# Attention's softmax sums: folded by small transfers and summed in the turn to queries, instead of by matmuls with ones

## The chip, the cores and the metric

The kernel runs on one core of a Trainium2 chip. The metric is the device time of one execution in microseconds (us), the median of several runs. The core has five engines that run side by side and meet through semaphores: TensorE (PE: matmuls, with PEld for its weight loads), VectorE (DVE), ScalarE (ACT), GpSimd (POOL) and SyncE (SP, which here only issues transfers). Each engine works through its own instructions strictly in order: an instruction that waits holds up all behind it. POOL and SP also issue transfers (DMAs), which 16 DMA engines carry out; a transfer that adds to its destination (an accumulate) is issued by POOL. SBUF is the working memory of 128 partitions, PSUM the memory that PE writes.

## The reference, cut to what matters

Two graph layers run one after the other over 16 batches of 1024 nodes with 256 features and a mask `adj`. The change touches the first one, attention with 8 heads of 32 features:

```python
normed = layer_norm(x, gamma1, beta1)
qkv = normed.reshape(b_, n_, H, HD).transpose(0, 2, 1, 3)
scores = jnp.einsum('bhqd,bhkd->bhqk', qkv, qkv) * scale
masked = jnp.where(adj_matrix[:, None, :, :] > 0, scores, -jnp.inf)
attn = jax.nn.softmax(masked, axis=-1)
out = jnp.einsum('bhqk,bhkd->bhqd', attn, qkv)
```

The softmax divides by a sum over 1024 keys. The kernel computes exp(scores) without division, weighs the values with it, and divides at the end by the sum. An MLP (1024 wide, GELU) and the second layer (single-head attention over the same mask, ELU) follow; together they are the "rest" below. All arithmetic that matters here is float32.

## The kernel before, in words

**Tiles.** In `attention` one batch is 32 *units*: 2 blocks of 512 queries (`qh`) x 2 sets of four heads (`g`) x 8 key tiles of 128 keys (`kt`). The eight units of one `(qh, g)` are called a *group* here, and a batch has four groups. In a unit `scores` lets PE write scores transposed, keys on the partitions and 4 heads x 512 queries along the row, into two PSUM tiles `sc0` and `sc1` (L990). These have one buffer each, so PE's next scores need DVE to have read the last ones. DVE adds the mask (L1011) and writes tile `e`, 128 x 2 x 512, once for each pair of heads; ACT takes the exponential (L1014). A unit later PE multiplies `e` with the values into `o` (`weigh`, L1027). At the last key tile DVE copies `o` to SBUF (L1042).

**The sums.** The first key tile's two `e` tiles are the accumulators `acc` (pool `accp`, two buffers each). For each further key tile `add_up` adds `e` to them by an accumulating DMA from POOL's queue (L1051), 512 KB each, two a unit. `e` tiles come from `ep`, with five buffers: one is free again when its accumulate has landed. After the last key tile each partition of `acc` holds a partial sum over 8 keys. `total` sums over the partitions: a matmul with ones gives, for head j, the sum in 32 rows of a PSUM tile `den` (L929), and ACT copies it to `ds` (L937). One unit later `invert` turns it to queries on partitions by small matmuls of `ds` with `each_head`, a matrix that picks one row of every 32 (L947), and DVE takes the reciprocal (L951). `finish` transposes `o` (L961) and DVE multiplies (L963). POOL adds the result to the residual `h` (L967). `finished[b, qh]` counts this.

In batch 0 PE adds the mask for two heads itself, and odd key tiles are summed by DVE in tiles `odd`; that path is not touched.

**The order of the work.** The order is written out by the program itself while it records instructions. Several generators ("streams") yield places on a common scale of batches, and the one with the lowest place goes next: attention (`stream_a`), the rest of the batch before (`stream_b`, one step of 1.75 us of PE work at a time), prologue, masks, set-up. `clock` is the program's own account of PE time. `defer(us, f)` records f once the clock has gone that far, which puts its instructions at that place in their engines' orders; it is no wait on the chip. `go_on` runs once a unit and hands each finished group on, a unit at a time: weighed, summed (`total`), totalled (`invert`). `turns` is a list of short PE jobs that are put in between steps.

`rest` does MLP and second layer in chunks of 256 queries: `expand` (ph, DVE L1184, GELU L1191), `contract` (po, L1211), then the second layer (`weights`: lg, DVE L1281 and L1286, ACT L1287; `attend`: pa, L1324 to L1334). The second half's chunks need `finished[b, 1]`; until then stream B yields without work. PSUM tiles other than `sc` and `o` share three buffers (`psm`).

**Other work on the queues.** POOL also computes `nrm` and `va` for the next batch (L815, L816), the small powers `rs` that DVE's normalisations need (L745), and the residual adds (L1127, L1128). SP issues all loads, the mask's transposes (L902) and the stores. DVE turns the loaded mask into FP8 (L592).

Of the kernel before, what the change touches and what calls it, by code (L numbers as in the profile page):

```python
# [9 lines left out]
F32 = mybir.dt.float32  # L10
# [4 lines left out]
ALU = mybir.AluOpType  # L15

P = 128
# [477 lines left out]
def fast_path(  # L495
# [28 lines left out]
    nc = tc.nc  # L524
    B, N, D = x.shape
    DFF = W1.shape[1]
    H, HD = 8, D // 8
    GH = 4
# [4 lines left out]
    QW = 512  # L533
# [7 lines left out]
    pool = lambda name, bufs, **kw: ctx.enter_context(tc.tile_pool(name=name, bufs=bufs, **kw))  # L541
    const = pool("const", 1)
# [6 lines left out]
    midp = pool("midp", 3)  # L549
    ep = pool("ep", 5)  # L550
    accp = pool("accp", 2)
    lp1 = pool("lp1", 6)
    tmpp = pool("tmpp", 2)
    smallp = pool("smallp", 3)
# [45 lines left out]

    each_head = const.tile([P, GH], F32, name="each_head")
    nc.vector.tensor_copy(each_head, ident[:, ::HD])
    ident8 = const.tile([P, P], FP8, name="ident8")
    nc.vector.tensor_copy(ident8, ident, saturate=False)
    ones = const.tile([P, HD], F32, name="ones")
# [152 lines left out]
    def defer(us, f):  # L758
        deferred.append((clock[0] + us, len(deferred), f))

        return clock[0] + us
# [160 lines left out]
    scored, weighed, summed, totalled = [], [], [], []  # L922

    def total(b, qh, g, os, accs):

        den = ps_tile([P, QW], f"den_{b}_{g}_{qh}")
        for j in range(GH):
            for acc in accs:
                nc.tensor.matmul(  # L929
                    den[j * HD : (j + 1) * HD, :],  # L930
                    ones,
                    acc[j // 2][:, j % 2, :],
                    start=acc is accs[0],
                    stop=acc is accs[-1],
                )
        ds = tmpp.tile([P, QW], F32, tag="w2", bufs=3, name=f"ds_{b}_{g}_{qh}")
        nc.scalar.copy(ds, den)  # L937
        totalled.append((b, qh, g, ds, os))

    finished = {}  # L940

    def invert(b, qh, g, ds, os):

        pt = ps_tile([P, TPH, GH], f"ptds_{b}_{g}_{qh}")
        for t in range(TPH):
            for c in range(0, P, HD):
                nc.tensor.matmul(  # L947
                    pt[c : c + HD, t, :], ds[:, t * P + c : t * P + c + HD], each_head, start=True, stop=True
                )
        rl = smallp.tile([P, TPH, GH], F32, tag="rl", name=f"rl_{b}_{g}_{qh}")  # L950
        ready = defer(1.0, lambda: nc.vector.reciprocal(rl, pt))  # L951
        turns.append((1, lambda: finish(b, qh, g, rl, ready, os)))
# [16 lines left out]
    def attention(b, st):  # L969
        va, kT = st["va"], st["kT"]  # L970

        def scores(qh, g, kt):
            qs = slice(qh * QW, (qh + 1) * QW)
            sc = [
                psc.tile([P, 2, QW], F32, tag=f"sc{i}", name=f"s_{b}_{g}_{qh}_{kt}_{i}") for i in range(2)
            ]

            by_pe = 2 if b == 0 else 0  # L980
            if by_pe:
                for j in range(by_pe):
                    matmul(
                        sc[j // 2][:, j % 2, :], ident8, st[qh][:, kt // 2, :, kt % 2], start=True, stop=False
                    )
                clock[0] += 0.45
            for j in range(GH):
                r = slice(j * HD, (j + 1) * HD)
                for c in range(0, P, P // 2):
                    nc.tensor.matmul(  # L990
                        sc[j // 2][c : c + P // 2, j % 2, :],
                        kT[r, g, kt * P + c : kt * P + c + P // 2],
                        kT[r, g, qs],
                        start=j >= by_pe,
                        stop=True,
                    )
            mb = st[qh][:, kt // 2, :, kt % 2].unsqueeze(1).to_broadcast([P, 2, QW])
            es = []
            if b == 0 and kt % 2:

                odd = midp.tile([P, 2, 2, QW], F32, tag="mid", name=f"odd_{g}_{qh}_{kt}")
            for i in range(2):
                if b == 0 and kt % 2:
                    e = odd[:, i]
                elif kt == 0:
                    e = accp.tile([P, 2, QW], F32, tag=f"acc{i}", name=f"acc_{b}_{g}_{qh}_{i}")
                else:
                    e = ep.tile([P, 2, QW], F32, tag="e", name=f"e_{b}_{g}_{qh}_{kt}_{i}")
                masked = sc[i]
                if 2 * i >= by_pe:  # L1010
                    nc.vector.tensor_tensor(e, masked, mb, op=ALU.add)  # L1011
                    masked = e
                es.append(e)
                weights = lambda e=e, masked=masked: nc.scalar.activation(e, masked, AF.Exp, scale=SCALE)  # L1014
                if i == 0:
                    weights()
            return es, weights

        acc = {}


        def weigh(qh, g, kt, es):
            if kt == 0:
                acc[g, qh] = pso.tile([P, QW], F32, tag="o", name=f"o_{b}_{g}_{qh}")
            o = acc[g, qh]
            for j in range(GH):
                nc.tensor.matmul(  # L1027
                    o[j * HD : (j + 1) * HD, :],
                    va[:, kt, (g * GH + j) * HD : (g * GH + j + 1) * HD],
                    es[j // 2][:, j % 2, :],  # L1030
                    start=(kt == 0),
                    stop=(kt == NT - 1),
                )
            if b == 0 and kt % 2:

                if kt > 1:
                    for n, (e, w) in enumerate(zip(es, odds[g, qh])):
                        defer(1.0 + 2.5 * n, lambda e=e, w=w: nc.vector.tensor_add(e, e, w))
                odds[g, qh] = es
            if kt == NT - 1:  # L1040
                c = tmpp.tile([P, QW], F32, tag="w2", bufs=3, name=f"os_{b}_{g}_{qh}")
                nc.vector.tensor_copy(c, o)  # L1042
                weighed.append((b, qh, g, c, [s[g, qh] for s in (sums, odds) if s]))

        sums, odds = {}, {}


        def add_up(qh, g, kt, e, i):
            if b == 0 and kt % 2:
                return  # L1050
            nc.gpsimd.dma_start(sums[g, qh][i], e, accum_op=ALU.add)  # L1051

        units = [(qh, g, kt) for qh in range(NQH) for g in range(NG) for kt in range(NT)]
        for u in units:
            make_turns()
            es, rest_of_weights = scores(*u)
            go_on()
            rest_of_weights()
            qh, g, kt = u
            if kt == 0:  # L1060
                sums[g, qh] = es
            else:
                for i in range(2):
                    defer(2.0 + 1.5 * i, lambda u=u, e=es[i], i=i: add_up(*u, e, i))
            scored.append((weigh, (*u, es)))
            yield
# [47 lines left out]
    def rest(b, st, tails):  # L1114
# [55 lines left out]
        def expand(c):  # L1170
            yield from wait_for(turn, c)
            hid = midp.tile([P, FC, CW], F32, tag="mid", name=f"hid_{b}_{c}")
            for f0 in range(0, FC, 2):
                ph = ps_tile([P, 2, CW], f"ph_{b}_{c}_{f0}")
                for i in range(2):
                    for dc in range(DC):
                        matmul(
                            ph[:, i, :],
                            w1[:, dc, (f0 + i) * P : (f0 + i + 1) * P],
                            yT[c][:, dc, :],  # L1180
                            start=(dc == 0),
                            stop=(dc == DC - 1),
                        )
                nc.vector.tensor_tensor(  # L1184
                    hid[:, f0 : f0 + 2, :],
                    ph,
                    b1c[:, f0 : f0 + 2].unsqueeze(2).to_broadcast([P, 2, CW]),
                    op=ALU.add,
                )
                yield 1.75, True  # L1190
            return hid, defer(1.0, lambda: nc.scalar.activation(hid, hid, AF.Gelu))  # L1191
# [153 lines left out]
        hid = {0: (yield from expand(0))}  # L1345
        ask(turn, 1)
        yield from tails[b]()
        while finished.get((b, 1), 0) < NG:
            yield 0.0, None
        prepare(b, st, 2)  # L1350
        load(2)
        hid[1] = yield from expand(1)
        ask(turn, 2)
        prepare(b, st, 3)
        yield from contract(0, hid[0])
        load(3)
        hid[2] = yield from expand(2)
        ask(turn, 3)
# [135 lines left out]
    while any(p is not None for p in places):  # L1494
        i = min((p, i) for i, p in enumerate(places) if p is not None)[1]
# [69 lines left out]
```

## Time and profile before

| what | value |
|---|---|
| median of 3 runs | 3469.32 us (3466.48 to 3476.8) |
| the profiled execution: its own time | 3465.53 us |
| its span, first to last instruction | 3463.8 us |
| mean granted PE clock | 0.998 |
| PE / DVE / ACT / POOL busy | 99% / 79% / 54% / 41% |
| accumulates acc<-e | 864 of 512 KB, median 6.2 us from issue to landing |
| matmuls den<-acc | 512 instructions, 592 ns each, several at once |

Reading the rows: a group of the profile has line, engine, operation, what it writes and reads, and the count; behind the bar stand busy us and mean ns of one, then how long the engine sat idle before, and what ended that. One float32 matmul of the program appears as two instructions, and a matmul with 32 columns of weights runs beside three others, so durations of single matmuls don't add up: PE's time is read from the start of one set to the start of the next. Line numbers are those of the kernel before.

### The profile page before, as it was taken

Reading aid. Unit: us, or ns where it says so; the run is one execution under the profiler, and the core shown is the slowest. Engines: PE = TensorE matmul, PEld = TensorE weight load, DVE = VectorE, ACT = ScalarE, POOL = GpSimd, SP = SyncE. Lnnn points to the kernel's source line nnn. Section 1 sums busy time; section 2 is a strip of 40 time slices with the busy share of each in tenths; the row PEclk is TensorE's granted clock in tenths of the full one; section 3 lists DMA queues with packets and bytes.
Section 4 is the critical chain, followed back from the end, with each engine's and each line's share of the span. In section 5 each row is a group of like instructions: output and inputs, shape, how many; then the busy total and the mean of one; then the engine's idle time right before and its main releaser. Section 6 shows DMA issues by size and latency. Waiting matters only on the chain. (4 is left out here: it accounts for less than half of the span.)

```text
span 3463.8 us, 119015 instructions
## 1 busy us (share of the span) xinstructions
PE 3421.5 (99%) x52478; PEld 1644.7 (47%) x52478; DVE 2751.4 (79%) x5194; ACT 1857.5 (54%) x2184; POOL 1416.9 (41%) x1708
## 2 busy tenths in 40 slices
PE   7999999999999999999999999999999999999998
PEld 2344444444444444444444444444444444444477
DVE  6888788787878878888887887878878788887754
ACT  5555555555555555555555555555555555555522
POOL 4443443434444344443444434344343443433220
PEclk9999999999999999999999999999999999999999
DMA  8799989999899998999999899998999989899730
GB/s 195 154 183 181 185 164 194 177 193 185 164 185 176 185 187 169 184 171 191 189 177 186 166 189 179 188 187 168 186 178 193 186 163 184 170 193 180 153 64 14
DMA packets 281902, 598.56 MB, mean 173 GB/s; under 512 B 94880, under 2 KB 130080, under 8 KB 281376
## 3 DMA queue, kind: packets, MB, share of 16 engines
q0 software_dynamic: 124416, 453.04, 71.5%
q1 hardware_dynamic: 156672, 137.56, 15.9%
q8 instruction: 414, 6.78, 0.8%
q14 instruction: 112, 0.92, 0.1%
q10 hardware_dynamic: 288, 0.26, 0.0%
HBM read 104.21 MB, written 16.78 MB: 35 GB/s over the span
## 5 line engine op out<-in xcount | busy, mean ns | idle before, releaser
L1014 ACT ACTIVATE e<-e 128x1024 f32<-128x1024 f32 x852 | 895.9, 1057 | 947.6 <-DVE e L1011 715.3
L1051 POOL DMA_DIRECT2D acc<-e x864 | 756.2, 891 | 1447.4 <-DMA acc<-e 664.6
L1011 DVE TENSOR_TENSOR e<-s,mk 128x1024 f32<-128x1024 f32 x852 | 1004.0, 1218 | 180.1 <-PE s L990 148.4
L990 PE MATMUL s<-kT 32*64 32x512 f32 x8192 | 577.3, 615 | 2.9 <-DVE odd L1011 2.9
L1027 PE MATMUL o<-e,va 128*32 128x512 f32 x3456 | 462.9, 606 | 2.1 <-ACT e L1014 2.1
L571 PE MATMUL pa<-gw,e 128*32 128x258 f32 x7648 | 454.3, 380 | 0.6 <-issue 0.6
L571 PE MATMUL lg<-fT,uT 128*32 128x256 f32 x7680 | 448.5, 379 | 0.0
L571 PE MATMUL ph<-yT,w 128*32 128x256 f32 x7808 | 448.5, 379 | 0.0
L571 PE MATMUL po<-w,hid 128*32 128x256 f32 x7680 | 440.5, 379 | 0.0
L571 PEld LDWEIGHTS ph<-yT,w 128*32 128x32 f32 x7808 | 259.8, 110 | 197.7 <-issue 42.5
L571 PEld LDWEIGHTS po<-w,hid 128*32 128x32 f32 x7680 | 250.2, 110 | 209.1 <-issue 61.6
L571 PEld LDWEIGHTS lg<-fT,uT 128*32 128x32 f32 x7680 | 258.4, 110 | 190.1 <-issue 38.9
L571 PEld LDWEIGHTS pa<-gw,e 128*32 128x32 f32 x7648 | 249.9, 110 | 202.5 <-issue 49.9
L1287 ACT ACTIVATE e<-e,shift 128x512 f32<-128x512 f32 x256 | 183.0, 717 | 186.0 <-DVE e L1286 161.2
L1281 DVE SCALAR_TENSOR_TENSOR e<-lg,gw,mk 128x256 f32<-128x256 f32 x512 | 223.2, 478 | 71.6 <-PE lg L571 61.1
L1184 DVE TENSOR_TENSOR hid<-ph,b1c 128x512 f32<-128x512 f32 x256 | 175.6, 688 | 85.6 <-PE ph L571 74.2
L1027 PEld LDWEIGHTS o<-e,va 128*32 128x32 f32 x3456 | 68.8, 108 | 354.0 <-issue 219.9
L1286 DVE SCALAR_TENSOR_TENSOR e<-e 128x512 f32<-128x512 f32 x256 | 196.6, 768 | 8.8
L1014 ACT ACTIVATE acc<-acc 128x1024 f32<-128x1024 f32 x124 | 131.0, 1057 | 129.0 <-DVE acc L1011 124.6
L990 PEld LDWEIGHTS s<-kT 32*64 32x64 f32 x8192 | 120.6, 130 | 162.8 <-issue 105.0
L1011 DVE TENSOR_TENSOR acc<-s,mk 128x1024 f32<-128x1024 f32 x124 | 146.1, 1218 | 20.8 <-PE s L990 20.6
L815 POOL TENSOR_TENSOR nrm<-nrm,g 128x256 f32<-128x256 f32 x128 | 113.3, 885 | 60.9 <-DVE nrm L749 60.9
(146 smaller groups left out, 3817.9 us busy)
## 6 DMA issues: line engine op xcount, KB each, us to landing
acc<-e POOLq DMA_DIRECT2D x864, 512.0 KB, 6.2
adj<-in_adj_dram SPq DMA_DIRECT2D x248, 256.0 KB, 5.6
h<-in_x_dram SPq DMA_DIRECT2D x64, 256.0 KB, 6.3
xb<-in_x_dram SPq DMA_DIRECT2D x128, 128.0 KB, 4.2
out_dram<-z SPq DMA_DIRECT2D x128, 128.0 KB, 4.0
adj<-in_adj_dram SPq DMA_DIRECT2D x4, 512.0 KB, 7.1
mk<-mq SPq DMA_TRANSPOSE x128, 6.4
w<-in_L_gnn_W_dram SPq DMA_DIRECT2D x2, 1024.0 KB, 9.6
```

Of the source, the lines that this page charges most:

```text
L571: nc.tensor.matmul(out[c : c + HD], lhsT[:, c : c + HD], rhs, start=start, stop=stop)
L815: nc.gpsimd.tensor_mul(nrm, nrm, g1)
L990: nc.tensor.matmul(sc[j // 2][c : c + P // 2, j % 2, :], kT[r, g, kt * P + c : kt * P + c + P // 2], kT[r, g, qs], start=j >= by_pe, stop= ...
L1011: nc.vector.tensor_tensor(e, masked, mb, op=ALU.add)
L1014: weights = lambda e=e, masked=masked: nc.scalar.activation(e, masked, AF.Exp, scale=SCALE)
L1027: nc.tensor.matmul(o[j * HD : (j + 1) * HD, :], va[:, kt, (g * GH + j) * HD : (g * GH + j + 1) * HD], es[j // 2][:, j % 2, :], start=(kt = ...
L1051: nc.gpsimd.dma_start(sums[g, qh][i], e, accum_op=ALU.add)
L1184: nc.vector.tensor_tensor(hid[:, f0 : f0 + 2, :], ph, b1c[:, f0 : f0 + 2].unsqueeze(2).to_broadcast([P, 2, CW]), op=ALU.add,)
L1281: nc.vector.scalar_tensor_tensor(e[:, j, :], lg[:, j, :], gw[:, kt, D : D + 1], st[c // 2][:, kt // 2, qs, kt % 2], op0=ALU.add, op1=ALU.add,)
L1286: nc.vector.scalar_tensor_tensor(e, e, ALPHA, e, op0=ALU.mult, op1=ALU.max)
L1287: ready = defer(2.5, lambda: nc.scalar.activation(e, e, AF.Exp, bias=shift))
```

## The change

For the groups of batches 1 to 14 and of the first query block of batch 15 (58 of 64), `total` is no longer called. `fold` takes its place. In `acc[0]` the lower 64 partitions get the upper 64 added, in `acc[1]` the other way round, each by one accumulating DMA of 64 partitions from POOL (`fold_halves`). Then each head's 32 partitions of a tile `part` are filled from its own quarter (`take_own`, four DMAs of 32 x 512 from SP) and get the other quarter added (`add_other`, four accumulating DMAs from POOL). `part` then holds 32 partial sums a head, and `invert` uses it in place of `ds`, with `head_of` in place of `each_head`: ones on the head's 32 rows, so that the small matmul that turns to queries also sums. The steps are deferred by 5, 12, 17 and 23 us of the program's clock.

In the same groups the second key tile (`kt == 1`) is added to `acc` by a POOL tensor add instead of a DMA. And in `rest` the second `expand` stands ahead of the wait for `finished[b, 1]`, and two pieces of the first `contract` ahead of the turn of chunk 2.

```diff
+    foldp = pool("foldp", 1)
...
+    head_of = const.tile([P, GH], F32, name="head_of")
+    nc.gpsimd.memset(head_of, 0.0)
+    for j in range(GH):
+        nc.gpsimd.memset(head_of[j * HD : (j + 1) * HD, j : j + 1], 1.0)
...
-        totalled.append((b, qh, g, ds, os))
+        totalled.append((b, qh, g, ds, os, each_head))
+
+    def folds(b, qh):
+        return 0 < b and (b < B - 1 or qh == 0)
+
+    def fold(b, qh, g, os, acc):
+
+        part = foldp.tile([P, QW], F32, tag="part", name=f"part_{b}_{g}_{qh}")
+        half = [slice(i * P // 2, (i + 1) * P // 2) for i in range(2)]
+        heads = [slice(j * HD, (j + 1) * HD) for j in range(GH)]
+
+        def fold_halves():
+            for i in range(2):
+                nc.gpsimd.dma_start(acc[i][half[i]], acc[i][half[1 - i]], accum_op=ALU.add)
+
+        def take_own():
+            for j in range(GH):
+                nc.sync.dma_start(part[heads[j]], acc[j // 2][heads[j], j % 2, :])
+
+        def add_other():
+            for j in range(GH):
+                nc.gpsimd.dma_start(part[heads[j]], acc[j // 2][heads[j ^ 1], j % 2, :], accum_op=ALU.add)
+
+        defer(5.0, fold_halves)
+        defer(12.0, take_own)
+        defer(17.0, add_other)
+        defer(23.0, lambda: totalled.append((b, qh, g, part, os, head_of)))
...
-    def invert(b, qh, g, ds, os):
+    def invert(b, qh, g, ds, os, head):
...
-                    pt[c : c + HD, t, :], ds[:, t * P + c : t * P + c + HD], each_head, start=True, stop=True
+                    pt[c : c + HD, t, :], ds[:, t * P + c : t * P + c + HD], head, start=True, stop=True
...
-                weighed.append((b, qh, g, c, [s[g, qh] for s in (sums, odds) if s]))
+                if folds(b, qh):
+                    fold(b, qh, g, c, sums[g, qh])
+                else:
+                    weighed.append((b, qh, g, c, [s[g, qh] for s in (sums, odds) if s]))
...
+            if kt == 1 and folds(b, qh):
+                nc.gpsimd.tensor_add(sums[g, qh][i], sums[g, qh][i], e)
+                return
             nc.gpsimd.dma_start(sums[g, qh][i], e, accum_op=ALU.add)
...
         yield from tails[b]()
+        hid[1] = yield from expand(1)
         while finished.get((b, 1), 0) < NG:
             yield 0.0, None
         prepare(b, st, 2)
         load(2)
-        hid[1] = yield from expand(1)
+        pieces = contract(0, hid[0])
+        yield next(pieces)
+        yield next(pieces)
         ask(turn, 2)
         prepare(b, st, 3)
-        yield from contract(0, hid[0])
+        yield from pieces
         load(3)
```

## The prediction, made before the result was known

> **What bounds the kernel now.** I read the page first, then PE's waits, then one batch's window, then short timelines of PE, GpSimd (POOL) and VectorE (DVE).
>
> ```profile
> PE 3421.5 (99%) x52478; PEld 1644.7 (47%) x52478; DVE 2751.4 (79%) x5194; ACT 1857.5 (54%) x2184; POOL 1416.9 (41%) x1708
> q0 software_dynamic: 124416, 453.04, 71.5%
> L1051 POOL DMA_DIRECT2D acc<-e x864 | 756.2, 891 | 1447.4 <-DMA acc<-e 664.6 <-ACT e L1014 446.6 <-issue 86.8
> ```
>
> Since a busy PE is not yet a bounding PE, the list of its waits decides:
>
> ```profile
> PE ptk L823 <- POOL va L816: 18.8, 4, 15.9
> PE s L990 <- DVE odd L1011: 2.9, 2, 2.0
> PE s L571 <- ACT acc L1014: 2.5, 2, 1.4
> ```
>
> Below these stand only entries of 2.1 us and less, so PE waits some 33 us in 3463.8, nearly all in the first batch. From then on every cut of PE work is worth its full length, until something makes PE wait. One batch is 216.1 us, 54.0 for each of its four groups (a group: one block of 512 queries, four heads, eight key tiles):
>
> ```profile
> 1787.55:2003.60 216.05, 216.05 (x3452) 102.17 (x3448) 178.00 (x332) 119.34 (x140) 90.76 (x110) 1.00 0.94 182
> ```
>
> The columns are PE, PEld, DVE, ACT and POOL busy, the granted clock, the DMA engines' busy share and GB/s. PE never pauses, the clock is full, but DVE is at 178 of 216 and the DMA engines are at 0.94: two resources stand close behind PE. The POOL row of the page shows why the second matters: 664.6 us of POOL's idle time is waiting for one accumulate (L1051) to land before the next into the same tile.
>
> **Part 1: the sums' matmuls (removed).** The changed program has total() only for the six groups that do not fold; 14 batches x 4 + 2 = 58 groups lose theirs. The cost is read from start to start:
>
> ```profile
> 682.13 1.06 PE L1027 MATMUL o<-e,va 128*32 128x512 f32 x8
> 683.01 1.04 PE L929 MATMUL den<-acc,ones 128*32 128x512 f32 x8
> 683.87 1.48 PE L571 MATMUL lg<-fT,uT 128*32 128x256 f32 x24
> ```
>
> 683.87 - 683.01 = 0.86 us, all on the path. 58 x 0.86 = 49.9 us gained. The copy of den on ACT (567 ns each) goes too and is worth nothing, ACT being 55% busy. The matmuls of invert() and finish() stay, one unit later (key tile 4 instead of 3): 0. The five new memsets at the start: under 0.5 us (the row of such a memset is 0.1), 0 taken.
>
> **Part 2: the new order in rest().** In the changed program's PE order only one pair of expand matmuls and the turn pty of chunk 2 move by a unit. They fill the place that ptds and ptos leave; PE's work is the same: 0. If the cover were gone, it would cost what PE waits for the second sums, which is part 4.
>
> **Part 3: the second key tile on POOL.** 58 x 2 = 116 accumulates become tensor adds of 128x1024. POOL's adds of 256 columns average 750 ns (L1128), those of 512 have a median of 1286, so 1024 take about 1286 + 2 x 536 = 2.36 us. POOL has the time (275 us more on 1417); the question is DVE.
>
> ```profile
> L1286 DVE SCALAR_TENSOR_TENSOR e<-e x256: 691/692/2056, 260.0 to 3446.7; 128x512 f32<-128x512 f32 x128
> L967 POOL TENSOR_TENSOR h<-h,ot x64: 1266/1286/2274, 67.3 to 3325.7; 128x512 f32<-128x512 f32 x64
> ```
>
> These are minimum, median and maximum. L1286 reads SBUF alone; where a POOL add runs beside it, it takes up to 2056 ns and the POOL op stretches too, while L1011, which reads PSUM, stays at 1218 throughout. So a 2.36 us add can hold L1286, L592, L1333 and L1334 for up to its length. The worst place that I found is the group (second queries, second heads):
>
> ```profile
> 1794.11 0.69 DVE L1286 SCALAR_TENSOR_TENSOR e<-e 128x512 f32<-128x512 f32 x1
> 1794.72 0.76 DVE L592 TENSOR_SCALAR mq<-adj 128x512 fp8e5<-128x512 int32 x2
> 1795.39 2.35 DVE L1011 TENSOR_TENSOR e<-s,mk 128x1024 f32<-128x1024 f32 x2
> ```
>
> With adds from about 1792.7 to 1798, L1286 slips in between them and L592 waits for the second. L1011 then starts near 1798.4 and ends near 1800.8. PE's next scores, which need it, started at 1800.31 and would now start 0.86 earlier: a PE wait of 1.3 us. In the group (first queries, first heads) no such DVE op falls under the adds: 0. (Second queries, first heads): 0 to 2, by whether a small DVE op gets in before the first add. (First queries, second heads): 0. So 1.3 to 3.3 us a batch.
>
> **Part 4: the fold closes a loop on POOL.** Today the first accumulate of a group goes to a fresh tile and waits for nobody's landing:
>
> ```profile
> 1749.26 0.85 POOL L1051 DMA_DIRECT2D acc<-e  x1 [1.69 <-ACT e L1287]
> 1752.85 0.85 POOL L1051 DMA_DIRECT2D acc<-e  x1 [2.73 <-ACT gw L1263]
> 1755.59 0.85 POOL L1051 DMA_DIRECT2D acc<-e  x1 [1.90 <-DMA acc<-e]
> ...
> 1785.61 0.86 POOL L1051 DMA_DIRECT2D acc<-e  x1 [2.43 <-DMA acc<-e]
> 1791.36 0.86 POOL L1051 DMA_DIRECT2D acc<-e  x1 [4.89 <-ACT e L1014]
> ```
>
> 1749.26 is the second accumulate of key tile 2, 1785.61 that of key tile 7: five steps in 36.35 us, 7.3 each, of which the landing of the step before takes 6.2 in the median (4.5 at least, 11.6 at most). In the changed order POOL waits, after key tile 7, for its landing; then issues the folds of halves, makes both adds, issues key tile 2's first accumulate, four add_other (which wait for SP's take_own, and that for the folds), and only then key tile 2's second accumulate. The loop is:
>
> - five steps 36.35 + last landing 6.2 = 42.5;
> - second fold 0.9, adds 4.7, one accumulate 0.9, four add_other at the row's 0.86 = 3.4: 9.9;
> - ordinary POOL work standing between them (none, one h/xb pair of 1.8, two pairs with a small pow of 0.7, four nrm/va with one): 0, 1.8, 4.3 and 4.3, mean 2.6;
> - sum 55.0 us a group, against PE's 54.0 - 0.86 = 53.1.
>
> So PE would wait 1.9 a group, at ptds, or where DVE wants an e tile that has not been added. The bounds: the small DMAs' issue is shown nowhere on POOL; SP's issues take 0.34, so four at that price (1.4 for 3.4), with landings at the 4.5 minimum and 0.5 from a landing to the next, make 5 x 5.0 + 4.5 + 7.9 + 2.6 = 40.0, no wait at all. Upward, the group (first queries, first heads), with more loads under way, needed 44.3 instead of 42.5 by the same reading: 56.8 in all, 3.7 a group. I take 1.2: nearest to the measured 55.0, less a part for the two accumulates a group that no longer crowd the engines (the 256 KB folds and 64 KB pieces move the same bytes, 1024 KB, but in POOL's pause). Part 3's waits lie in the same groups, before ptds, and are contained in it: a PE that has waited at the scores finds the sums landed. 58 x 1.2 = 70 us lost.
>
> SP's queue: take_own stands before h loads, transposes and stores, and holds them some 4 us; their use is more than a unit (5.5 us) away: 0, and if not, DVE would wait at L592.
>
> The Trainium skill speaks against the small transfers: "DMA: Bandwidth & Descriptors", Rules for kernel authors, has transfers under 64 KB as mostly overhead. Its section Anatomy of one DMA gives 2.0 us + bytes/436e3, an estimate of 3.2 us for 512 KB where this trace's median is 6.2; by it the loop would be near 34 us and nothing would be lost. The measured landing decides.
>
> **The sum.** -49.9 + 70 = +20 on the profiled execution (3465.5 us; span 3463.8 and 1.7 around it): 3485.6. The median of the runs lies 3.8 above that execution: 3489.
>
> **Rivals.**
> - *The loop closes in time* (faster). Small DMAs cost POOL little and landings shorten, the loop stays under 53; only DVE's blocks are left, 14.5 batches x 1.3 to 3.3 = 19 to 48, of which I count 15, because DVE's 38 idle us of a batch let it catch up where POOL's adds start early: -49.9 + 15 gives 3434 beside the median, from 3420 with nothing lost. For it: the DMA engines idle in the pause, 1447 us of POOL idle. It decides once the turn from one group's last landing to the next group's second accumulate is under 10.6 us.
> - *POOL and its DMAs become the bound.* 1.9 a group and more, up to 3.7: 58 x 1.9 = 110, so 3529; 58 x 3.7 gives 3634.
> - *A draw*: 0.7 to 1.0 a group, 3459 to 3479.
> - That den would not go is excluded by the changed program's PE order.
>
> **How the numbers follow.** A measurement here tells 0.3% (10 us) from no change. Chances: mild loss (3480 to 3515) 0.36, loop closes 0.35, draw 0.13, POOL-bound (over 3515) 0.16. Faster 0.35, same 0.13, slower 0.52. The point is the mild loss's 3489; the range for 8 in 10, 3428 to 3550, cuts about a tenth at each end.
>
> **What would show it.** Right: L929 with some 48 matmuls on acc; PE waits at ptds or s, near 1.2 us a group; L1286's and L592's means up; the folds' first issue behind a DMA wait; POOL near 57% busy. Wrong: PE's waits still some 33 us (then 3420 to 3435), landings of accumulates well under 6.2, or small DMAs that cost POOL far less than 0.86.

## The result, and the profile after

The changed kernel takes 3693.2 us in the median of four runs (3675.6 to 3705.2) against 3469.6 for the kernel before: a ratio of 1.064, with an interval of 1.059 to 1.068. It is slower, as forecast, but by 224 us where 20 were named, and 143 us above the upper end of the range. The profiled execution took 3694.6 us with a span of 3692.8. Ratios below leave out one slow execution (3746.1 us, of the first kernel that moves ptds), which that kernel's median still holds.

The page of the changed kernel, engines and the lines that answer to those shown before (L1088 is the accumulate that was L1051):

```profile
PE 3468.7 (94%) x52014; PEld 1680.0 (45%) x52014; DVE 2893.1 (78%) x5194; ACT 1835.0 (50%) x2126; POOL 1881.9 (51%) x2061
q0 software_dynamic: 128128, 437.85, 67.4%
L1088 POOL DMA_DIRECT2D acc<-e x748 | 738.7, 1000 | 1273.5 <-DMA acc<-e 588.2
```

PE has 464 instructions less, which are the 58 x 8 of the sums, and should be busy 50 us less. It is busy 47 us more, and stands still for 224.1 us of the span instead of 42.3. PE's waits say where:

```profile
PE ptds L978 <- DMA part<-acc: 117.2, 42, 8.4
PE ptk L828 <- POOL va L821: 18.6, 4, 15.6
PE pg L572 <- ACT uT L1285: 15.0, 11, 3.0
PE s L1021 <- DVE e L1042: 14.2, 18, 2.0
```

The columns are us in all, times, and the longest. The names are PSUM tiles: ptds is the turn of the sums to queries, ptos that of `o`, s the scores, ptk the keys of the next batch; pg, ph, pty, ptf and puT belong to `rest`. The entry at ptds is new and the largest: PE has come to the turn of the sums before the last 64 KB pieces have landed. One such wait in windows (PE, PEld, DVE, ACT and POOL busy, granted clock, DMA share, GB/s):

```profile
1585.00:1588.00 3.00, 3.00 (x44) 0.85 (x36) 2.90 (x11) 2.42 (x4) 2.95 (x4) 1.00 0.86 169
1588.00:1592.00 4.00, 0.17 (x13) 0.15 (x13) 2.90 (x4) 2.11 (x2) 1.62 (x2) 0.90 1.10 258
1592.00:1598.00 6.00, 6.00 (x88) 3.45 (x91) 2.06 (x8) 3.19 (x2) 0.00 (x0) 0.50 1.43 139
1598.00:1602.00 4.00, 4.00 (x72) 2.38 (x64) 2.88 (x9) 0.43 (x1) 1.59 (x2) 0.99 1.00 88
```

PE pauses for 3.83 us up to 1591.88, and then works for six us at a clock of 0.50. So this wait is paid nearly twice. Over the span the mean clock is 0.979 instead of 0.998: 0.021 x 3692.8 = 78 us lost to it against 7 before. Part of that falls into the pauses themselves; while PE works, half clock costs 62 us against 5. From PE's side the sum is: 50 gained by the matmuls, 182 lost in pauses (224.1 - 42.3), 58 in half clock at work, 39 in PE time that I can't assign; 229, the difference of the spans.

From the other side, POOL's line of work in the same group (start, length, idle time before and what ended it):

```profile
1563.84 0.86 POOL L1088 DMA_DIRECT2D acc<-e  x1 [1.30 <-ACT acc L1045]
...
1568.65 0.84 POOL L956 DMA_DIRECT2D acc<-acc  x1
1570.53 0.81 POOL L956 DMA_DIRECT2D acc<-acc  x1 [1.04 <-DMA acc<-e]
...
1572.87 4.94 POOL L1086 TENSOR_TENSOR acc<-acc,e 128x1024 f32<-128x1024 f32 x2
...
1582.05 0.71 POOL L750 TENSOR_TENSOR rs_a<-ve_a,mhalf 128x2 f32<-128x2 f32 x1 [2.55 <-DVE ve_a L748]
1582.72 0.89 POOL L1088 DMA_DIRECT2D acc<-e  x1
1583.34 3.69 POOL L964 DMA_DIRECT2D part<-acc  x4
1585.34 2.61 POOL L1088 DMA_DIRECT2D acc<-e  x1
```

This is the loop of the prediction's step 4: last accumulate, wait for its landing, folds, adds, first accumulate of key tile 2, the four pieces, second accumulate. I read its three parts from the events of 48 groups (batches 2 to 13), in the mean: second accumulate of key tile 2 to that of key tile 7, 37.7 us; its landing, 6.3; from there to the next group's second accumulate of key tile 2, 12.8. Together 56.8 us. PE's groups, from one first weighing to the next, average 56.7. The two must agree, since the three parts end on the instruction on which they began, one group later: the same instants in the kernel before give 36.0, 6.5 and 10.2, 52.8 in all. So the parts show where a group has grown, 2.5 us in the turn and 1.6 in the steps, and not yet what bounds it. In the five steps POOL stands still for 20.7 of 37.7 us, 9.6 of them until an accumulate has landed and 4.7 until ACT has an exponential ready.

The same spacing in the kernel before is not what the prediction said. The first weighing of a group and the same one a batch later:

```profile
1788.59 1.06 PE L1027 MATMUL o<-acc,va 128*32 128x512 f32 x8
...
1999.43 1.06 PE L1027 MATMUL o<-acc,va 128*32 128x512 f32 x8
```

A batch takes 210.8 us, and 52.7 to 52.8 a group over the run, not 216.1 and 54.0: the window that I took for a batch was 5.2 us too long.

### The profile page after: what moved, and what is told of

It reads as the page before. It is cut to its first block, busy times and chain, and to the rows that moved or that the text cites. A ratio compares the mean times of both kernels' runs of the same rounds, so it can differ in the third digit from the quotient of the medians.

```text
span 3692.8 us, 119248 instructions
## 1 busy us (share of the span) xinstructions
PE 3468.7 (94%) x52014; PEld 1680.0 (45%) x52014; DVE 2893.1 (78%) x5194; ACT 1835.0 (50%) x2126; POOL 1881.9 (51%) x2061
## 2 busy tenths in 40 slices
DMA packets 296754, 598.59 MB, mean 162 GB/s; under 512 B 102304, under 2 KB 137504, under 8 KB 296224
## 5 line engine op out<-in xcount | busy, mean ns | idle before, releaser
L1088 POOL DMA_DIRECT2D acc<-e x748 | 738.7, 1000 | 1273.5 <-DMA acc<-e 588.2
L1042 DVE TENSOR_TENSOR e<-s,mk 128x1024 f32<-128x1024 f32 x852 | 1005.0, 1216 | 169.3 <-PE s L1021 108.2
L1021 PE MATMUL s<-kT 32*64 32x512 f32 x8192 | 605.0, 616 | 20.2 <-DVE e L1042 14.2
L572 PE MATMUL po<-w,hid 128*32 128x256 f32 x7680 | 473.5, 399 | 0.0
L572 PE MATMUL lg<-fT,uT 128*32 128x256 f32 x7680 | 457.0, 384 | 0.0
L572 PEld LDWEIGHTS po<-w,hid 128*32 128x32 f32 x7680 | 268.9, 116 | 214.4 <-issue 83.0
L572 PEld LDWEIGHTS lg<-fT,uT 128*32 128x32 f32 x7680 | 275.1, 111 | 171.1 <-issue 43.1
L1086 POOL TENSOR_TENSOR acc<-acc,e 128x1024 f32<-128x1024 f32 x116 | 286.8, 2549 | 3.4 <-ACT e L1045 3.4
L1323 DVE SCALAR_TENSOR_TENSOR e<-e 128x512 f32<-128x512 f32 x256 | 257.9, 1008 | 8.8
L1221 DVE TENSOR_TENSOR hid<-ph,b1c 128x512 f32<-128x512 f32 x256 | 174.1, 686 | 78.4 <-PE ph L572 66.3
L964 POOL DMA_DIRECT2D part<-acc x232 | 198.8, 1420 | 14.7 <-DMA part<-acc 10.1
```

The lines of the kernel that those rows point to most:

```text
L572: nc.tensor.matmul(out[c : c + HD], lhsT[:, c : c + HD], rhs, start=start, stop=stop)
L964: nc.gpsimd.dma_start(part[heads[j]], acc[j // 2][heads[j ^ 1], j % 2, :], accum_op=ALU.add)
L1021: nc.tensor.matmul(sc[j // 2][c : c + P // 2, j % 2, :], kT[r, g, kt * P + c : kt * P + c + P // 2], kT[r, g, qs], start=j >= by_pe, stop= ...
L1086: nc.gpsimd.tensor_add(sums[g, qh][i], sums[g, qh][i], e)
L1221: nc.vector.tensor_tensor(hid[:, f0 : f0 + 2, :], ph, b1c[:, f0 : f0 + 2].unsqueeze(2).to_broadcast([P, 2, CW]), op=ALU.add,)
L1323: nc.vector.scalar_tensor_tensor(e, e, ALPHA, e, op0=ALU.mult, op1=ALU.max)
```

## The experiments

All are edits of the changed kernel unless said otherwise. Each comparison is with the kernel before on the same chip, whose medians lay at 3471 to 3475 us. Three causes were on the table, with letters that changed on the way. Latency (A, later L): PE reaches ptds too early. Throughput (B): the loop on POOL is longer than PE's group. Held DVE (C, later H): POOL's adds hold VectorE. D was the DMA engines' time as such.

**Each part by itself.** The fold without the adds:

```diff
-            if kt == 1 and folds(b, qh):
-                nc.gpsimd.tensor_add(sums[g, qh][i], sums[g, qh][i], e)
-                return
```

> The changed kernel, but the second key tile is accumulated by a DMA as before; the fold stays. Theory A: the fold's four landings stay one behind the other, and add_other now stands behind an accumulate that waits for key tile 1's landing (about 6 us) instead of behind 4.8 us of adds: 3650 to 3760, PE's wait at ptds 100 us or more. Theory B: as A, since the loop is not shorter: 3650 to 3720. Theory C: VectorE is freed, the mean of L1323's operation falls from 1008 ns to about 770, and the time falls to 3450 to 3550.

Measured: 3729.1 us, ratio 1.072 (1.069 to 1.074); PE waits 208.8 us at ptds. So the fold loses on its own, and more than with the adds.

The same three lines put into the kernel before, with nothing else:

> The kernel before with nothing changed but the second key tile of the 58 folding groups added by GpSimd; sums, total() and ptds as before. Theories A and B: the adds alone cost little, 3455 to 3490 us (at most the 1.3 to 3.3 us a batch of my step 3). Theory C: 3550 to 3690, PE's waits at the scores behind VectorE.

Measured: 3539.5 us, ratio 1.019 (1.017 to 1.020), some 66 us slower. That is above what A and B gave and below C, and PE waits for something that no theory named:

```profile
PE ph L571 <- ACT ds L937: 23.4, 14, 1.7
PE puT L571 <- ACT ds L937: 18.8, 13, 1.5
```

The same moments on DVE, POOL and ACT, from three timelines of that run:

```profile
1503.77 4.86 DVE L749 TENSOR_SCALAR ft<-xb,mv_d,rs_d 128x256 f32<-128x256 f32 x2
1508.55 1.83 DVE L592 TENSOR_SCALAR mq<-adj 128x512 fp8e5<-128x512 int32 x2
```

```profile
1503.72 4.76 POOL L1052 TENSOR_TENSOR acc<-acc,e 128x1024 f32<-128x1024 f32 x2 [1.29 <-ACT e L1014]
```

```profile
1511.54 1.06 ACT L1014 ACTIVATE e<-e 128x1024 f32<-128x1024 f32 x1 [6.95 <-DVE e L1011]
1512.50 0.57 ACT L937 COPY ds<-den 128x512 f32<-128x512 f32 x1
```

Two normalisations of 0.41 us each take 2.47 beside adds of 2.4 and end within 0.2 us of these. The mask add behind them comes late, so does ACT's exponential, and behind that in ACT's queue the copy that frees den's PSUM tile, for which PE's next matmuls wait. Over the 116 adds, DVE operations that overlap one lose 109 us against their usual length: L749 62, the other half on two further lines (L1289, which is the L1286 of before, 24, and L743 23). The prediction had L1286 but neither of the other two.

The new order in `rest` alone, in the kernel before:

> The kernel before with only part 2, the new order in rest(): PE's work is the same and only moved by a unit. My step 2 and all theories: no difference, 3460 to 3480. If the order itself made PE wait, 3490 and more.

Measured: 3477.9 us, ratio 1.0018 (1.0003 to 1.0033): within what the measurement tells from nothing, as step 2 had it. What the order is worth inside the changed kernel was not run.

**Whether the length of one add is what DVE pays.** In the kernel with the adds alone:

```diff
-                nc.gpsimd.tensor_add(sums[g, qh][i], sums[g, qh][i], e)
+                for r in range(2):
+                    for c in range(0, QW, 256):
+                        s = (slice(None), r, slice(c, c + 256))
+                        nc.gpsimd.tensor_add(sums[g, qh][i][s], sums[g, qh][i][s], e[s])
```

> The kernel with the adds alone (no fold), each add of 128x1024 cut into four of 128x256. Theory C in the form that the trace of that run suggests: a VectorE operation that reads and writes SBUF alone stands still until the running GpSimd add ends (the normalisation L749 took 2.47 us beside an add of 2.44, 0.41 without); with short adds it is held for 0.75 us at most, and the 66 us fall to 15 to 35: 3485 to 3505 us. If GpSimd's share of the port and not the length of one operation decides: unchanged or slower, 3535 and more.

Measured: 3477.9 us, ratio 1.0012 (1.0000 to 1.0024). The 66 us are gone but for some 4. The normalisation in the lists of operations of the two runs, first with whole adds, then with cut ones:

```profile
L749 DVE TENSOR_SCALAR ft<-xb,mv_d,rs_d 128x256 f32<-128x256 f32 x128 | 108.9, 893 | 6.5 <-POOL rs_d L745 6.3
```

```profile
L749 DVE TENSOR_SCALAR ft<-xb,mv_d,rs_d 128x256 f32<-128x256 f32 x128 | 59.7, 508 | 0.4 <-POOL rs_d L745 0.4
```

893 ns fall to 508 (413 in the kernel before), although POOL now spends 347 us on the adds, 782 ns apiece. So it is the length of the single operation, and not POOL's time, that the kernel pays for. DVE is not wholly free: its operations that overlap an add still lose 57 us in all (L592 30 of them), but in pieces short enough for the run to lose 4.

**Moving ptds.** First by one and by two units, in all groups:

```diff
-        defer(23.0, lambda: totalled.append((b, qh, g, part, os, head_of)))
+        defer(29.0, lambda: totalled.append((b, qh, g, part, os, head_of)))
```

> The changed kernel with ptds one unit later (the last step of the fold deferred by 29 instead of 23). Theory A, latency: PE comes to ptds before the last 64 KB piece has landed, since accumulate of key tile 7, folds, take_own and add_other follow one another with about 18.5 us from the first landing to the last, and PE gets there too early; each pause of 2 us and more also costs 1.7 to 3.4 us of half clock. Then nearly all of the 117 us at ptds and of the 71 us of clock go: 3440 to 3520 us, granted clock 0.99 or more. Theory B, throughput: the loop of accumulates and folds on GpSimd is itself longer than PE's group, so that the wait only moves, to the scores or to later sums: 3600 to 3690. Theory C, VectorE is held by GpSimd's adds: no change by moving ptds, 3650 to 3700.

> The changed kernel with ptds two units later (35 instead of 23). Theory A: no wait at ptds is left, 3420 to 3500, at or below the version with one unit. Theory B: 3600 to 3690, PE's waits now at the scores or at a place that waits for VectorE's e tiles. Theory C: 3650 to 3700.

Measured: 3715.4 (1.0635, 1.0605 to 1.0666) and 3712.0 us (1.0676, 1.0658 to 1.0694). The wait at ptds was gone and the time was not. These two don't decide, though, for the edit did more than it says: `rest` waits for the last group of a batch, and with that one later its work piled up in later units (with 35 in place of 29, two units of a batch had none of it and a later one more than twice its share). The largest new waits of the first stand there:

```profile
PE ptos L992 <- DVE nm L802: 58.1, 14, 7.8
PE pty L1194 <- DVE y L754: 49.1, 15, 4.7
```

So the last group of a batch kept its place, and the other three went two units later:

```diff
+        last = (qh, g) == (NQH - 1, NG - 1)
-        defer(23.0, lambda: totalled.append((b, qh, g, part, os, head_of)))
+        defer(23.0 if last else 35.0, lambda: totalled.append((b, qh, g, part, os, head_of)))
```

> The changed kernel with ptds two units later for three groups of four; the group (second queries, second heads) keeps its place, because in the two versions before the work of rest() that waits for it ran dry. Theory A, latency: three of the four waits at ptds vanish with their half clock: 3480 to 3580 us. Theory B, throughput: the loop of accumulates, folds and small pieces on GpSimd takes some 56 to 57 us a group whatever PE waits at, against PE's 51.9; then the mean length of a group stays at 56 or more and the time at 3630 to 3720, with PE's waits at other places.

Measured: 3669.5 us, ratio 1.056 (1.052 to 1.060), 24 us better than the changed kernel, with intervals that just touch. PE's waits of that run:

```profile
PE ptf L1271 <- DVE ft L754: 36.5, 18, 7.2
PE s L1022 <- DVE e L1043: 35.8, 36, 7.8
PE pg L572 <- ACT uT L1286: 29.6, 14, 3.3
PE ptk L828 <- POOL va L821: 18.3, 4, 15.4
PE ptds L979 <- DMA part<-acc: 10.3, 8, 2.9
```

The 117 us at ptds have shrunk to 10, and new waits stand elsewhere. DVE's waits show how they get there:

```profile
DVE ft L754 <- POOL rs_d L750: 91.7, 22, 9.8
DVE e L1043 <- PE s L1022: 85.4, 105, 2.8
DVE e L1043 <- DMA acc<-e: 68.6, 52, 10.6
```

DVE lacks a free `e` tile because the accumulates are behind (4.2 us of this before, 38.2 in the changed kernel, 68.6 here), and it waits for the powers `rs`, which stand in POOL's queue behind waits for landings. The loop's three parts are 37.5, 6.5 and 12.3 us here, 56.2 in all: 0.6 less. So a group stays as long with the wait at ptds gone, as B had it. That it is the chain on POOL that keeps it long is for the next runs to show.

**Another order on POOL.** In the three groups the whole fold later, so that POOL needn't stand for key tile 7's landing:

```diff
-        defer(5.0, fold_halves)
-        defer(12.0, take_own)
-        defer(17.0, add_other)
+        defer(5.0 if last else 14.5, fold_halves)
+        defer(12.0 if last else 22.0, take_own)
+        defer(17.0 if last else 26.5, add_other)
...
+        defer(23.0 if last else 40.0, lambda: totalled.append((b, qh, g, part, os, head_of)))
```

> As the version with three late groups, but in these three groups GpSimd also issues the folds and the small pieces later (folds deferred by 14.5, take_own by 22, add_other by 26.5, ptds by 40), so that it doesn't stand still for the landing of key tile 7 and of take_own before it goes on with the next group's accumulates. The same work, the same bytes, another order on its queue. Theory B: the loop of three groups shortens by the landing of key tile 7 and the fold's wait, 10 us and more, and falls below PE's group; what is left is the cost of the adds on VectorE and one unimproved group a batch: 3480 to 3570. Theory A: as for the version without the new order, no difference between the two. Theory D, the DMA engines have no time left for this many transfers in whatever order: 3630 or more.

> As the version with the new order on GpSimd's queue, but the second key tile goes by DMA as in the kernel before. Theory B: the loop has one step of about 7 us more but VectorE is not held: 3450 to 3560. Theory D: 61 MB more through DMA engines that were busy at 0.94 before, 3640 to 3750.

Measured: 3793.5 (1.093, 1.089 to 1.096) and 3917.7 us (1.125, 1.119 to 1.131). I was wrong here. Folds, pieces and the loads on SP's queue now fall among the accumulates, and all of them land later: accumulates after 6.4 us instead of 6.1 in the first run, folds after 5.6 instead of 5.1. The median from issue to landing of take_own, in the changed kernel and then in this order:

```profile
part<-acc SPq DMA_DIRECT2D x232, 64.0 KB, 2.2
```

```profile
part<-acc SPq DMA_DIRECT2D x232, 64.0 KB, 6.2
```

POOL now stands at add_other for 66.3 us until take_own has landed (10.1 in the changed kernel), with key tiles 3 to 7 behind it; how much of the loss that is, no run separates. The first time lies in the range that D gave, but its DMA engines are busy 0.88 to 0.89 of the time between 1200 and 2000 us, less than the 0.92 to 0.93 of the kernel before. With 61 MB more (the second run) they are busy 0.97 to 0.98 over two batches in the middle; D may have a part in that one.

**Taking steps out of the loop.** These kernels leave key tiles out of the sums. Tile 3:

```diff
+            if kt == 3 and folds(b, qh):
+                return
```

> The changed kernel, but the exponentials of key tile 3 are left out of the sums of the folding groups (the output is therefore not the reference's): one step of the chain of accumulates less, the adds, the folds and the small pieces as they are. Theory B: the loop shortens by one step of about 7.2 us, from some 56.6 to 49.4 us a group, below PE's 51.9, so that the waits for the sums go and with them the half clock; what remains is the cost of the adds on VectorE, 66 us by the run with the adds alone: 3469 - 50 + 66 = 3485, between 3460 and 3540. If the loop is not what binds (the order of the work, SyncE's queue, the pieces themselves): above 3620.

Measured: 3603.8 us, ratio 1.036 (1.034 to 1.038), 90 us better than the changed kernel and 119 above what B alone gave, so inside neither case. PE still waits at ptds:

```profile
PE ptds L978 <- DMA part<-acc: 96.4, 31, 5.4
```

So latency seems a bound too, once a step is out of the chain. Leaving the tile out also takes 61 MB from the DMA engines, so D is not excluded by this run. Tile 1, and tiles 1 and 3:

> The changed kernel with key tile 1 left out of the sums of the folding groups, so without GpSimd's adds, and with six accumulating steps as in the changed kernel. Theory B: GpSimd stands for the folds' and take_own's landing during most of the 4.8 us that the adds took, so the loop shortens by 0 to 4.8 us: 52 to 56 us a group, and 3470 to 3660. The difference to the changed kernel is what the adds cost inside it; if they cost their full 66 us beside the loop, 3627 or less.

> The changed kernel with key tiles 1 and 3 both left out of the sums of the folding groups: no adds, five steps, folds and pieces as they are. Theory B: a loop of some 46 to 49 us, nothing waits for it, VectorE is not held: 3469 - 50 = 3419, between 3400 and 3450, with PE's waits near those of the kernel before. If the folds or the pieces cost something of their own beside the loop, 3460 and more.

Measured: 3551.2 (1.021, 1.019 to 1.023) and 3461.5 us (0.9969, 0.9956 to 0.9982). Without the adds 142 us come back, more than the 66 that they cost by themselves; a group is 2.7 us shorter, 1.4 of it in the turn, where the adds stood. With both tiles out the time is 42 us above the 3419 that the matmuls promised, in the second case that had been named, a cost of folds or pieces beside the loop; 24.3 us of waits at ptds are left in it, the rest was not traced. Even with five of seven steps the fold hardly pays.

**Two causes at once.** Tile 3 left out and three groups late:

> The changed kernel with uncut adds, key tile 3 left out of the sums of the folding groups (the output is not the reference's), and ptds late for three groups. L and a step of B are taken away, H is left. If H alone then acts, as in the run with the adds alone: 3469 - 50 + 66 = 3485, 3470 to 3530. If it stays above 3570, the held VectorE operations lengthen the loop itself.

Measured: 3495.4 us, ratio 1.0057 (1.0041 to 1.0074), 10 above the 3485 expected. PE's longest waits are now:

```profile
PE ptk L828 <- POOL va L821: 18.6, 4, 15.6
PE pg L572 <- ACT uT L1288: 18.5, 14, 2.1
PE s L1022 <- DVE e L1043: 7.8, 8, 2.6
```

The first is the start-up wait that the kernel before has. Later ptds alone gave 24 us, one step less alone 90, both 198: two bounds of nearly the same length, each of which hides the other. By subtraction, what remains is the 66 us of the held DVE, less the 50 of the matmuls, and 10 more; DVE's operations that overlap an add do lose 134 us in this run, against 109 in the kernel with the adds alone.

Cut adds in the changed kernel, cut adds with late ptds, and tiles 1 and 2 both by cut adds with late ptds:

> The changed kernel with each GpSimd add of 128x1024 cut into four of 128x256, nothing else. Three causes are on the table: L, the fold's last piece lands after PE has come to ptds; B, the loop of accumulates and folds is longer than PE's group; H, VectorE's SBUF-only operations stand still for the whole length of an add. Without the adds at all the changed kernel took 3551. If H is what the adds cost, this lands there too, between 3540 and 3600; if the adds cost by GpSimd's time in the loop, 3640 and more.

> As the version with cut adds, and ptds two units later for three groups of four. L and H are both taken away, B is left. If the loop of GpSimd then still takes longer than PE's 51.9 us a group: 3520 to 3600, as without the late ptds. If the loop was long only because held VectorE work and pauses of PE fed back into it: 3430 to 3500.

> As before, but key tiles 1 and 2 are both added by GpSimd in cut adds, so that five accumulating steps remain; ptds late for three groups. L, H and a step of the loop are taken away, and 61 MB from the DMA engines; the output is the reference's. If the three causes are the whole loss, this is the kernel before without the 50 us of den's matmuls and with a few us of holds: 3425 to 3465, faster than both. If GpSimd itself is now too full (12.4 us of adds a group): 3500 and more.

Measured: 3712.3 (1.068, 1.064 to 1.073), 3683.1 (1.060, 1.056 to 1.065) and 3629.7 us (1.044, 1.041 to 1.048). The first and the third land in the second of their cases, where GpSimd's time counts; the second misses both of its own. Cutting eases DVE, but a group's cut adds take POOL 5.9 us instead of 4.9 (342.4 and 286.8 us busy over 58 groups), and they stand in the turn: what cured the kernel with the adds alone leaves the changed one no faster (1.068 against 1.064, intervals that overlap). Two key tiles on POOL shorten the chain of accumulates by a step and bring the adds to 12.7 us a group (738.7 us busy over 58). This run also answers D for the loop: it moves 61 MB less, its DMA engines are busy only 0.79 to 0.80 of the time between 1200 and 2000 us, and a group still takes 55.8 us.

At last the adds on VectorE, one unit later, with late ptds, and then add_other later too:

```diff
-                nc.gpsimd.tensor_add(sums[g, qh][i], sums[g, qh][i], e)
+                nc.vector.tensor_add(sums[g, qh][i], sums[g, qh][i], e)
...
-        defer(17.0, add_other)
+        defer(17.0 if last else 24.0, add_other)
```

> The changed kernel with key tile 1 added by VectorE (one unit later in its queue) instead of GpSimd, and ptds two units later for three groups. L is away, H is away, and the adds' 4.9 us are out of GpSimd's turn between two groups; VectorE has 58 x 2 operations of about 1.2 us more, 140 us, and stands at some 84%. GpSimd's turn still waits for the folds and for take_own, about 11 us, so a loop of 36.5 + 6.3 + 11 = 54 us against PE's 51.9: 3470 to 3550. If the loop only binds with the adds in it: 3420 to 3460.

> As the version with VectorE's adds, and add_other issued about 7 us later (24 instead of 17, ptds at 38) in three groups, so that the second accumulate of key tile 2 no longer stands behind pieces that wait for take_own. If that standing is what keeps the loop above PE's group, three groups fall to 52 us: 3425 to 3475, the first version that might beat both. If the pieces now stand in the way of key tile 3 or 4 instead, as in the version with all of the fold later: 3500 or more.

Measured: 3611.7 (1.037, 1.034 to 1.042) and 3632.2 us (1.046, 1.041 to 1.051). The first misses, the second lands in its second case. With adds of 1249 ns on DVE, no hold and no wait at ptds, a group still takes 55.3 us: 37.5 for five steps, 6.3 for the landing, 11.5 for the turn. And 58 x (55.3 - 51.9) - 50 is 147, near the 137 that this kernel loses. POOL stands still for 5.3 us of that turn, most of it for data from ACT, PE and DVE, so POOL's own work doesn't explain this group's length by itself; what does, stays open. With add_other later the turn falls to 10.4 and the steps grow to 39.2: what the one gained, the other lost. PE has a new wait there, too:

```profile
PE ptos L993 <- DVE rl L983: 60.2, 14, 8.2
```

No version here that computes the reference beats the kernel before.

## Why the prediction was right and wrong

**What bounds the kernel.** Right that PE bounds it and that every cut of PE's work counts until something makes PE wait. Wrong in the length of a batch, 216.1 for 210.8; so PE's group after the change is 52.8 - 0.9 = 51.9, not 53.1.

**Part 1, the matmuls.** Right: 464 instructions fewer. In the run with key tiles 1 and 3 left out PE's busy time, at a clock of 0.998, is 3375.7 us against 3421.5, 46 less for the 50 forecast.

**Part 2, the order in rest().** Right: 1.0018.

**Part 3, the adds.** POOL's price was near (2.55 us measured, 2.36 estimated). The cost to PE was 66 us by itself, 4.5 a batch where I had 1.3 to 3.3. In that kernel what failed is the list of operations at risk: I took only those that I could see stretched, and left out the normalisations L749, which were its largest item. In the changed kernel the list holds better: of the 116 us that operations beside an add lose there, L1323 (the L1286 of before) has 45 and L593 (L592) 33, and L754, the normalisations, 10. The Trainium skill had the missing item: in "SBUF — State Buffer", section Who interferes with whom, VectorE and GpSimd share a port pair that one instruction holds to its end, and operations of the kind tensor_scalar, copies and casts can take it with a single SBUF input, in their two-port modes. These runs agree: 2.47 us beside an add of 2.4, 0.41 without, and the mask add L1011, which reads PSUM, at 1218 ns in the mean before and 1216 after. That part 3's waits are contained in part 4 can be judged only in part: the run with both bounds lifted lies where some 66 us of them would still be paid (3495 against 3485).

**Part 4, the loop.** The mechanism was right, and this is the main point of the case: waits at ptds, and a chain on POOL that closes from group to group. The step that failed is its price, 1.2 us a group: PE's groups take 56.7 us, 4.8 above the 51.9 that PE's own work needs. Three things make it up. I set the sum against a group of PE that was 1.2 us too long, which is 58 x 1.2 = 70 us. From the remaining 1.9 I took 0.7 off, 41 us, for accumulates that would no longer crowd the engines; nothing of the kind happened, the median landing went from 6.2 to 6.1. And the loop is 56.8 instead of 55.0, 104 us: five steps 37.7 for 36.35, landing 6.3 for 6.2, turn 12.8 for 12.5. Together that is 215 us, where the miss is 204.

The turn is near in part by luck. The four pieces hold it up for 2.0 us, not for 3.4: above, the first starts at 1583.34 and the next accumulate at 1585.34, while their 3.5 us of busy time run on beside it. And some 2 us in which POOL stands still, half of it until ACT has an exponential ready, were not in the sum. By my own 55.0 and the right group the sum is 58 x (55.0 - 51.9) - 50 = 130, so 3600, still 93 short. My upper reading of 56.8 gives 58 x 4.9 - 50 = 234, against 224 measured; but it was read from one group with more loads under way, and that the mean of all groups came out the same is luck. The sum also had one bound where the runs show two: with the loop a step shorter, ptds alone still held PE for 96.4 us.

**What the working left out.** The half clock after a pause, 58 us of PE's working time more than before, had no term; I had "the clock is full" from the kernel before. "TensorE: Matmul & The Clock Gate", Part 1, describes it: an idle window of about 3.4 us halves the clock, and a busy one restores it. Here the stretches of half clock at ptds are 3.4, 6.8 or 10.2 us long, and cost at most half of that, 1.7, 3.4 or 5.1 us each, which agrees. All 17 pauses at ptds of 3.2 us and more had one begin within them or up to 0.7 us behind; but 3 of the 10 between 1.7 and 2.6 us, shorter than the page's window, were followed by one too. Whether the half clock lengthened the run on top of the loop, or only filled time in which PE would have waited, no run separates.

**The rivals.** The one that came true was that POOL and its DMAs become the bound, which had 0.16; its end of 3634 is 59 us short. SP's queue was costed at 0, with take_own holding it for some 4 us. Fourteen of them stand far longer, until an accumulate has landed:

```profile
SPq L960 <- DMA acc<-e: 452.0, 14, 38.0
```

What SP's loads lose by it is small as far as DVE tells, whose wait for `adj` grew from 13.8 to 25.6 us; no run isolates it.

**The signs named.** PE's waits at ptds: yes, 117.2 us, which is 2.0 a group instead of 1.2. The folds' issue behind a landing: yes, 177 us at 89 of the 116. DVE's means: the L1286 of before, now L1323, went from 768 to 1008 ns, L592 from 469 to 618. POOL at 51% instead of 57%.

## What to carry to other kernels

When a chain on a queue closes into a loop, its sum against the bounding engine's period is the first forecast, and both need the same care: take the period from the same instruction in two successive rounds, count the waits inside the loop, and don't discount a measured sum for a relief that no row shows. A transfer that replaces PE's work must be free not only in bytes but in its place: work ordered behind a landing on a queue that all groups share makes the groups follow one another, where before they overlapped. And two bounds of nearly equal length hide each other, so an experiment that lifts one and gains little has not cleared it.

## What the runs showed that I had not expected

In PE's account a pause costs nearly a third more than its length: 182 us more of pauses, 58 us more of half clock at work. A GpSimd add cut into four costs more of POOL's time (2.95 us against 2.47 busy in the changed kernel), and in the kernel with the adds alone it still takes nearly all of their cost away. The bytes that the DMA engines moved did not change (598.56 and 598.59 MB): the adds took 1 MB of accumulates a group off them, and the fold's smaller transfers put the same total back, in 5% more packets.

Open: the kernel with key tile 1 left out has 54.1 us a group and the one with VectorE's adds 55.3, with the same work on POOL; and what share of a step's 7.5 us is the DMA engines' load, at 0.88 to 0.94 of the time, and what a fixed delay. Neither was told apart.
